# A decoder in one program: layer 2's self attention with heads split over two row groups, and layer 3's block quantisation in 16-bit pieces with a written order

## The chip, the cores and the metric

The kernel runs on one core of a Trainium2 chip. The core has five engines that work side by side, each through its own queue in order: PE (matrix multiplication; PEld is its loading of weights), DVE and ACT (element-wise work), POOL, and SP (here it only issues DMAs). SBUF is the on-chip memory of 128 partitions, PSUM the memory that PE writes. The metric is the device time of one execution in microseconds, lower is better. It was 2435.77, the median of three (2435.06 to 2436.54).

## The reference

The program computes a decoder of four layers on x of 8 blocks (b), 112 tokens and 256 features, in float32. Each layer has a self attention, a cross attention and a feed-forward part (FFN), each added to x. Two of the twelve parts matter here.

Layer 2's self attention has 8 query heads and 4 key and value heads of width 128, rotary positions and a causal mask:

```python
q = (hidden_states @ Wq).reshape(b, t, NH, D).transpose(0, 2, 1, 3)
k = (hidden_states @ Wk).reshape(b, t, NKV, D).transpose(0, 2, 1, 3)
v = (hidden_states @ Wv).reshape(b, t, NKV, D).transpose(0, 2, 1, 3)
q = q * cos + _rotate_half(q) * sin        # (-x2, x1): the halves of a head swapped
k = k * cos + _rotate_half(k) * sin
attn = jnp.einsum('bhtd,bhsd->bhts', q, k) * scale   # k, v repeated for two heads each
attn = jax.nn.softmax(jnp.where(causal, -jnp.inf, attn), axis=-1)
out = jnp.einsum('bhts,bhsd->bhtd', attn, v)
return out.transpose(0, 2, 1, 3).reshape(b, t, NH * D) @ Wo
```

Layer 3's FFN multiplies quantised values: every 16 neighbours share a scale that is rounded to an 8-bit float, and the values are rounded to eight magnitudes and a sign. Inputs and weights both are quantised so, and the hidden values once more (256 to 1024 to 256 features):

```python
amax = jnp.max(jnp.abs(xb), axis=-1, keepdims=True)          # xb: blocks of 16
sc8 = jnp.clip(amax / FP4_MAX * global_scale, 0.0, FP8_MAX).astype(float8_e4m3fn)
dq = sc8.astype(jnp.float32) / global_scale
a = jnp.clip(jnp.abs(xb) / jnp.where(dq == 0.0, 1.0, dq), 0.0, FP4_MAX)
q = jnp.sign(xb) * _FP4_VALS[jnp.digitize(a, _FP4_MIDS)]
return q * dq
...
hidden = silu(linear(x, gate_w)) * linear(x, up_w)
return linear(hidden, down_w)        # linear quantises both operands
```

## The kernel before

One class holds x in SBUF (tokens on partitions, S = 112, blocks along the free axis) through the whole program; the parts run one after the other (`SUBLAYERS`). A half is four blocks (HB = 4, HT = 448 tokens). Weights come through a ring of buffers by DMAs on SP's queue. Where nothing else is said, the Tile framework's scheduler sets the order of the instructions on each engine, within the limits of data and buffers, so that work of neighbouring parts interleaves; under `tc.manual_schedule` the order on the engines named is that of the code.

**Layer 2's self attention** (`l2_attn`, L1463 to L1512). `ln_T` normalises x and transposes it to xnT (features on partitions). Then for each half: `out` is qT (8 heads) or kT (4 heads), one chunk c of 128 partitions for each head. A chunk is a product mm of 128x448 (L407), two multiplications by sin which read the one half of the partitions and write the other (`rot`, L1487), one by cos (L1490), and POOL's addition of the two (L1491). Then each of the four blocks b: values vb, and in two groups g of four heads the scores sc (L407), mask addition, maxima and subtraction on DVE (L494, L496, L497), the exponential on ACT (L498), row sums (L1518, L1519), transposes of e (L506), the weighted values av, token-major, scaled into o (L1509), transposes of o into oT (L530), and after both groups the product with Wo and the addition to x (L484). PSUM tiles mm, sc, tr and av have two buffers each.

**The next part** (`l2_xattn`) normalises x into x1 (L445), multiplies by a gain and adds a bias (L1529, L1530, on DVE and POOL), and normalises and transposes x1. x1 stands in SBUF where qT of `l2_attn` stood, so it is written only when that tile is free.

**Layer 3's quantisation** (`quantise`, L1968) works on n values of a row, 16 neighbours a block: block maxima (L1985), nine operations on the n/16 scales (L1987 to L2001), multiplication by the inverse scale (L2004), clamping (L2005), the power of two below each value (L2007, L2008), rounding by adding and subtracting a large number (L2009, L2010), and multiplication by the scale into bfloat16 (L2011). Everything else is float32. It is used by `l3_weights` for the three weight matrices, which is dealt out as a generator inside layer 2's FFN (2048 values a row, in two calls of 1024), and by `l3_ffn` (L2060 on): on the normalised x of each half (1024 wide, result xq), and on the hidden values of two blocks at a time (2048 wide, hid into hq). Around it `l3_ffn` has the products gu (gate and up), silu on ACT (sg), hid on DVE (L2104), transposes of hq (L2113), a copy (hqT, L2117), the product y with the down weights, and the addition to x (L2121). `l0_attend` of layer 0 already works with heads of width 64 on two row groups of PE and with a written order; its lines L730 to L783 are named below because of that.

## Time and profile before

| | us |
|---|---|
| median of three runs | 2435.77 |
| lowest, highest | 2435.06, 2436.54 |
| the profiled execution, device time | 2432.16 |
| its span in the trace | 2430.4 |
| PE, DVE, ACT, POOL busy | 2138.1, 1434.3, 826.8, 215.8 |
| mean granted clock of PE | 0.954 |

All rows of the profile come from the one profiled execution; its span begins with the first and ends with the last recorded instruction. A row of the groups names line, engine, operation, output and inputs, shapes, count, busy time and mean duration, and then the engine's idle time ahead of that group with what ended it. PE's instructions overlap, so a mean duration of PE is longer than the distance from one start to the next.

### The profile page before, as it was taken

Reading aid. Unit: us, or ns where it says so; the run is one execution under the profiler, and the core shown is the slowest. Engines: PE = TensorE matmul, PEld = TensorE weight load, DVE = VectorE, ACT = ScalarE, POOL = GpSimd, SP = SyncE. Lnnn points to the kernel's source line nnn. Section 1 sums busy time; section 2 is a strip of 40 time slices with the busy share of each in tenths; the row PEclk is TensorE's granted clock in tenths of the full one; section 3 lists DMA queues with packets and bytes.
Section 4 is the critical chain, followed back from the end, with each engine's and each line's share of the span. In section 5 each row is a group of like instructions: output and inputs, shape, how many; then the busy total and the mean of one; then the engine's idle time right before and its main releaser. Section 6 shows DMA issues by size and latency. Waiting matters only on the chain.

```text
span 2430.4 us, 43101 instructions
## 1 busy us (share of the span) xinstructions
PE 2138.1 (88%) x17032; PEld 1268.6 (52%) x17032; DVE 1434.3 (59%) x3810; ACT 826.8 (34%) x2220; POOL 215.8 (9%) x415
## 2 busy tenths in 40 slices
PE   6999999889899899899988859899999999899842
PEld 3444444455556566546555536466555556556622
DVE  4555556565446567553877547767740223667698
ACT  2333334453312356430111213467321111346521
POOL 0111111000011100000222331100000000100000
PEclk9999999999999999999999979999999999899966
DMA  4000000000100000100001011000111100000000
GB/s 185 2 2 2 2 20 35 29 18 18 52 1 15 18 1 2 36 26 18 35 18 35 18 28 52 17 2 19 53 35 62 41 1 1 1 1 2 2 1 15
DMA packets 10729, 55.93 MB, mean 23 GB/s; under 512 B 1833, under 2 KB 3625, under 8 KB 5792
## 3 DMA queue, kind: packets, MB, share of 16 engines
q1 hardware_dynamic: 8304, 44.57, 5.1%
q0 software_dynamic: 2080, 7.07, 0.9%
q8 instruction: 135, 2.21, 0.4%
q10 hardware_dynamic: 144, 1.54, 0.2%
q14 instruction: 66, 0.54, 0.1%
HBM read 52.23 MB, written 0.92 MB: 22 GB/s over the span
## 4 chain that ended last, share of the span: by engine, by line
PE 66%; DVE 22%; issue 5%; ACT 4%; DMA 2%; POOL 1%; DVEq 0%; ACTq 0%; POOLq 0%
PE mm L407 31%; PE tr L1178 6%; PE gu L407 6%; PE g L640 6%; PE sc L407 4%; PE av L1194 3%; PE tr L407 1%; DVE rot L1487 1%; PE av L777 1%; ACT sg L651 1%; PE av L407 1%; ACT th L662 1%; PE s L407 1%; DVE hT L666 1%; DMA cx<-in_ctx 1%
## 5 line engine op out<-in xcount | busy, mean ns | idle before, releaser
L640 PE MATMUL g<-w,hT 128*32 128x256 f32 x3552 | 237.4, 384 | 26.0 <-DVE hT L666 24.6
L1178 PEld LDWEIGHTS tr<-cst,xe 112*125 112x125 f32 x1152 | 151.5, 188 | 96.7 <-issue 37.0
L1165 DVE TENSOR_REDUCE xnm<-sc 112x1 f32<-112x375 f32 x384 | 184.3, 540 | 29.5 <-PE sc L407 28.9
L1178 PE MATMUL tr<-cst,xe 112*125 112x112 f32 x1152 | 193.1, 289 | 8.6 <-DVE xeT L1186 3.5
L407 PE MATMUL mm<-xnT,w 128*128 128x448 f32 x432 | 183.0, 559 | 19.7 <-DVE qT L1490 4.5
L407 PE MATMUL mm<-hT,w 128*128 128x448 f32 x512 | 193.0, 539 | 0.0
L640 PEld LDWEIGHTS g<-w,hT 128*32 128x32 f32 x3552 | 95.7, 109 | 167.5 <-DVE hT L666 124.6
L407 PEld LDWEIGHTS mm<-hT,w 128*128 128x128 f32 x512 | 97.1, 190 | 94.4 <-issue 94.4
L1186 DVE COPY xeT<-tr 125x336 f32<-125x336 f32 x192 | 97.3, 507 | 70.4 <-PE tr L1178 63.0
L618 PE MATMUL g<-xw,cst 128*32 128x256 f32 x1792 | 138.7, 379 | 0.0
L1184 ACT COPY xeT<-tr 125x336 f32<-125x336 f32 x192 | 85.0, 443 | 155.8 <-PE tr L1178 155.8
L407 PE MATMUL mm<-w,hT 128*112 128x256 f32 x576 | 132.6, 389 | 0.0
L407 PEld LDWEIGHTS mm<-xnT,w 128*128 128x128 f32 x432 | 77.8, 193 | 102.8 <-issue 52.6
L1169 ACT ACTIVATE xe<-sc,xnm 112x375 f32<-112x375 f32 x256 | 126.2, 581 | 9.5 <-DVE xnm L1165 9.2
L407 PE MATMUL mm<-w,oT 128*112 128x256 f32 x416 | 105.8, 405 | 24.0 <-DVE oT L1667 15.2
L407 PE MATMUL gu<-xnT,w 128*128 128x448 f32 x320 | 124.4, 544 | 1.7 <-DVE hT L1332 1.2
L407 PEld LDWEIGHTS mm<-w,hT 128*112 128x112 f32 x576 | 103.7, 182 | 27.5 <-issue 4.8
L651 ACT ACTIVATE sg<-g 128x192 f32<-128x192 f32 x224 | 73.9, 330 | 105.4 <-PE g L640 94.1
L662 ACT ACTIVATE th<-cell 128x64 f32<-128x64 f32 x224 | 57.5, 257 | 147.2 <-DVE cell L660 147.1
L407 PEld LDWEIGHTS mm<-w,oT 128*112 128x112 f32 x416 | 73.9, 186 | 54.1 <-DVE oT L1667 16.3
L664 DVE TENSOR_TENSOR h<-sg,th 128x64 f32<-128x64 f32 x224 | 50.4, 225 | 84.8 <-ACT th L662 84.8
L2046 DVE COPY wq<-tr 128x256 bf16<-128x256 bf16 (+1 forms) x12 | 4.6, 420 | 157.5 <-PE tr L2045 157.5
(398 smaller groups left out, 3673.3 us busy)
## 6 DMA issues: line engine op xcount, KB each, us to landing
w<-in_w SPq DMA_DIRECT2D x33, 1024.0 KB, 4.9
raw<-in_wq POOLq DMA_DIRECT2D x3, 1024.0 KB, 5.3
w<-in_w SPq DMA_DIRECT2D x3, 896.0 KB, 6.4
wi<-in_wint POOLq DMA_DIRECT2D x3, 768.0 KB, 5.6
w<-in_w SPq DMA_DIRECT2D x2, 768.0 KB, 4.2
ctxT<-in_ctxT ACTq DMA_DIRECT2D x1, 1500.0 KB, 8.3
cx<-in_ctx POOLq DMA_DIRECT2D x1, 1500.0 KB, 22.5
w<-in_w SPq DMA_DIRECT2D x2, 512.0 KB, 3.5
```

Source lines behind the costliest of these rows:

```text
L407: self.nc.tensor.matmul(out, lhsT, rhs, start=i == 0, stop=i == len(pairs) - 1)
L618: nc.tensor.matmul(g[32 * j : 32 * j + 32, :], pick[:, t % 16, :], xw[:, l, t // 16, 256 * j : 256 * j + 256], start=True, stop=t == 0, sk ...
L640: nc.tensor.matmul(g[32 * j : 32 * j + 32, :], hT[l][:, c, :], whh[l][:, c, 256 * j : 256 * j + 256], start=False, stop=c == 1, skip_group ...
L651: nc.scalar.activation(sg[:, :192], g[:, :192], AF.Sigmoid)
L662: nc.scalar.activation(th, cell[l], AF.Tanh)
L664: nc.vector.tensor_tensor(h, og, th, ALU.mult)
L1165: nc.vector.tensor_reduce(nm, sc, AX.X, ALU.max, negate=True)
L1169: nc.scalar.activation(e, sc, AF.Exp, bias=nm)
L1178: nc.tensor.transpose(tp[:CH, i * S : (i + 1) * S], e[:, i * CH : (i + 1) * CH], self.ident[:S, :S])
L1184: nc.scalar.copy(eT, src)
L1186: nc.vector.tensor_copy(eT, src)
L1194: nc.tensor.matmul(avs[b][32 * j : 32 * j + 32, c * S : (c + 1) * S], values[b % 2][:CH, i, 4 * c + j, :], eTs[b, c, j][:, i, :], start=i ...
```

## The change

Two functions change their method; `l3_weights` and `_pack` on the host follow.

In `l2_attn` the columns of Wq and Wk are reordered on the host, so that a chunk of 128 partitions holds the first halves of two heads (x = 0), and the next chunk their second halves (x = 1). The rotation then combines two chunks without changing partitions, six DVE operations for a pair of chunks, with no POOL work; cos and sin for the queries are scaled by 1/sqrt(128) beforehand. A head's score is the sum of two products over 64 partitions, those of one head in partitions 0 to 63 and of the other in 64 to 127, into separate PSUM tiles (s0 to s3); the mask is added by a bfloat16 product with a unit matrix. DVE takes negated maxima; ACT's exponential takes them as bias and sums its rows; e is divided before it is transposed. Weighted values are computed feature-major (av), so that they need no transpose before the product with Wo. The order of PE, DVE and ACT is written out: half 0's six pairs stand in block 0, half 1's are dealt out in the half-steps after it, and a block's weighted values and result follow one and two blocks later. The helpers that only `l2_attn` used (`softmax_rows`, `heads_T`, `scores`, `out_T`, `self_psum`, `divided`, `row_sums`) go.

In layer 3 a block of 16 neighbours is laid out with a distance of k between its values (the host reorders the hidden features and the weights to match, and the normalisation writes xn in that order). Block maxima become a tree of four maxima over |values|, which ACT computes (Abs, `mag`); the scale s16 is bfloat16; after the multiplication the upper 16 bits of each float32 value, with the lowest bit set, are taken as bfloat16, and clamping, powers of two and rounding work on these; the result is written in two halves. `quantise` is a generator whose steps `l3_ffn` interleaves, in a written order, with the next blocks' products and the last blocks' additions to x. Weight maxima (amax in `l3_weights`) are read with the new strides.

```diff
+def _rotary(w):
+    n = w.shape[1] // P
+    a = w.reshape(w.shape[0], 2, 2, n // 4, 2, 64)
+    return a.transpose(0, 1, 3, 4, 2, 5).reshape(w.shape)
...
-        ("sin", np.concatenate([sin, -sin])),
+        ("sin", np.concatenate([sin, sin])),
...
+            def pair(half, l, i):
+                cols = slice(half * HT, (half + 1) * HT)
+                out, m = ((kT, wk), (qT, wq))[l]
+                cos, sin = turns[l]
+                parts = []
+                for x in range(2):
+                    pm = self.t(ps, [P, 512], "tr")[:, :HT]
+                    c = slice((2 * i + x) * P, (2 * i + x + 1) * P)
+                    self.mm(pm, [(m[:, k, c], self.xnT[:, k, cols]) for k in range(2)])
+                    parts.append(pm.rearrange("p (b s) -> p b s", b=HB))
+                a, b = (out[:, i, x, cols].rearrange("p (b s) -> p b s", b=HB) for x in range(2))
+                ra, rb = (self.t(acts, [P, HB, S], f"rot{x}") for x in range(2))
+                nc.vector.tensor_tensor(a, parts[0], cos, ALU.mult)
+                nc.vector.tensor_tensor(rb, parts[0], sin, ALU.mult)
+                nc.vector.tensor_tensor(ra, parts[1], sin, ALU.mult)
+                nc.vector.tensor_tensor(b, parts[1], cos, ALU.mult)
+                nc.vector.tensor_tensor(a, a, ra, ALU.subtract)
+                nc.vector.tensor_tensor(b, b, rb, ALU.add)
...
+            def score(b, p):
+                cols = slice(b * S, (b + 1) * S)
+                for r in range(2):
+                    scs[b, p, r] = self.t(ps1, [P, 512], f"s{2 * p + r}")[:S, : 2 * S].rearrange("p (h t) -> p h t", h=2)
+                    nc.tensor.matmul(
+                        scs[b, p, r].rearrange("p h t -> p (h t)"), ident, mask.rearrange("p h t -> p (h t)"),
+                        start=True, stop=False, skip_group_check=True,
+                    )
+                for i in range(2):
+                    for x in range(2):
+                        for r in range(2):
+                            rows = slice(64 * r, 64 * r + 64)
+                            nc.tensor.matmul(
+                                scs[b, p, r][:, i, :], qT[rows, 2 * p + i, x, cols], kT[rows, p, x, cols],
+                                start=False, stop=x == 1, skip_group_check=True,
                             )
-                        nc.vector.tensor_tensor(dst, src, cos, ALU.mult)
-                        nc.gpsimd.tensor_tensor(dst, dst, rot, ALU.add)
-                for j in range(HB):
-                    b = half * HB + j
-                    cols = slice(j * S, (j + 1) * S)
-                    vb = self.t(work, [P, 4, P], "vb")
-                    pm = self.t(ps, [P, 512], "mm")[:S]
-                    self.mm(pm, [(x, wv[:, k, :]) for k, x in enumerate(self.tokens(b))])
-                    self.cp(vb[:S], pm.rearrange("p (h d) -> p h d", h=4))
-                    o = self.t(work, [P, 8, P], "o")
-                    for g in range(2):
-                        hs = range(g * 4, g * 4 + 4)
-                        sc = self.scores(ps, [(qT[:, h, cols], kT[:, h // 2, cols]) for h in hs])
-                        e = self.softmax_rows(sc, work, 4, scale, self.c("causal"))
-                        ri = self.row_sums(e, 4)
-                        eT = self.heads_T(e, work, ps, 4)
-                        av = self.t(ps, [P, 512], "av")[:S].rearrange("p (h d) -> p h d", h=4)
-                        for i, h in enumerate(hs):
-                            self.mm(av[:, i, :], [(eT[:, i, :], vb[:S, h // 2, :])])
-                        nc.vector.tensor_tensor(
-                            o[:S, g * 4 : g * 4 + 4, :], av, ri[:, :, None].to_broadcast([S, 4, P]), ALU.mult
+            def maxima(b, p):
+                if p == 0:
+                    nms[b] = self.t(work, [P, 8], "nm")[:S]
+                    sus[b] = self.t(work, [P, 8], "su")[:S]
+                for r in range(2):
+                    at = 4 * p + 2 * r
+                    nc.vector.tensor_reduce(nms[b][:, at : at + 2], scs[b, p, r], AX.X, ALU.max, negate=True)
+            def exponent(b, p):
+                es[b, p] = self.t(work, [P, 4, S], f"e{p}")[:S]
+                for r in range(2):
+                    for i in range(2):
+                        h = slice(4 * p + 2 * r + i, 4 * p + 2 * r + i + 1)
+                        nc.scalar.activation(
+                            es[b, p][:, 2 * r + i, :], scs[b, p, r][:, i, :], AF.Exp,
+                            bias=nms[b][:, h], accum_out=sus[b][:, h],
                         )
-                    oT = self.out_T(o.rearrange("p h d -> p (h d)"), work, ps, 1024)
-                    self.add_to_x(b, self.project(ps, b, oT, wo))
+                    del scs[b, p, r]
+            def divide(b, p):
+                ri = self.t(self.small, [P, 4], "ri4")[:S]
+                nc.vector.reciprocal(ri, sus[b][:, 4 * p : 4 * p + 4])
+                nc.vector.tensor_tensor(es[b, p], es[b, p], ri[:, :, None].to_broadcast([S, 4, S]), ALU.mult)
...
+            def attend(b, p):
+                eT = eTs.pop((b, p))
+                av = self.t(ps1, [P, 512], "av")[:, : 4 * S]
+                for r in range(2):
+                    at = slice(2 * r * S, (2 * r + 2) * S)
+                    nc.tensor.matmul(
+                        av[:, at], vbs[b][:, 2 * p + r, :], eT[:, at], start=True, stop=True, skip_group_check=True
+                    )
+                if p == 0:
+                    oTs[b] = self.t(work, [P, 2, 4 * S], "oT")
+                (nc.vector.tensor_copy, nc.scalar.copy)[p](oTs[b][:, p, :], av)
+            def result(b):
+                oT = oTs.pop(b).rearrange("p a (i s) -> p (a i) s", i=4)
+                out = self.t(ps1, [P, 512], "mm")[:S, :D]
+                self.mm(out, [(oT[:, c, :], wo[:, c, :]) for c in range(8)])
+                self.add_to_x(b, out)
+            with tc.manual_schedule(engines={ET.PE, ET.DVE, ET.Activation}):
+                for _ in norm(0):
+                    pass
+                now = prepare(0)
+                later = chain(norm(1), prepare(1))
+                for b in range(NB + 2):
+                    on, last = b < NB, 0 < b <= NB
+                    for p in range(2):
+                        if b == 0:
+                            for _ in range(3):
+                                next(now)
+                        if on:
+                            score(b, p)
+                            maxima(b, p)
+                        if last:
+                            turn(b - 1, p)
+                        if on:
+                            exponent(b, p)
+                        if p == 0:
+                            if b > 1:
+                                result(b - 2)
+                        elif on:
+                            value(b)
+                        next(later, None)
+                        if last:
+                            attend(b - 1, p)
+                        if on:
+                            divide(b, p)
         w.done("l2a_wo")
...
+    def block_max(self, pool, src, rows, n, row):
+        nb, k = n // 16, row // 16
+        e, a = 16, src.rearrange("p (r e k) -> p r e k", e=16, k=k)
+        while e > 1:
+            e //= 2
+            out = self.t(pool, [P, nb * e], f"qm{nb * e}")[:rows]
+            o = out.rearrange("p (r e k) -> p r e k", e=e, k=k)
+            self.nc.vector.tensor_tensor(o, a[:, :, :e, :], a[:, :, e : 2 * e, :], ALU.max)
+            a = o
+        return out
...
+            amax = self.block_max(pool, mag, rows, n, row)
+            yield
+        sc, st, z, s16 = sm("s"), sm("t"), sm("z"), sm("h", BF16)
         nc.vector.tensor_scalar(sc, amax, 1.0 / 6.0, gs, ALU.mult, ALU.mult)
         nc.vector.tensor_scalar(sc, sc, 448.0, None, ALU.min)
@@ -1994,21 +2080,34 @@
         )
         nc.vector.tensor_scalar(st, st, 0.125 * big, 2.0**-9 * big, ALU.mult, ALU.max)
         nc.vector.tensor_tensor(sc, sc, st, ALU.add)
-        nc.vector.tensor_tensor(sc, sc, st, ALU.subtract)
-        nc.vector.scalar_tensor_tensor(z, sc, 0.0, sc, ALU.is_equal, ALU.add)
+        nc.vector.tensor_tensor(s16, sc, st, ALU.subtract)
+        nc.vector.scalar_tensor_tensor(z, s16, 0.0, s16, ALU.is_equal, ALU.add)
         nc.vector.reciprocal(z, z)
         nc.vector.tensor_scalar(z, z, gs, 1.0 + 2.0**-23, ALU.mult, ALU.mult)
+        yield
         a = self.t(pool, [P, n], f"qa{n}")[:rows]
-        m = self.t(pool, [P, n], f"qm{n}")[:rows]
-        nc.vector.tensor_tensor(blocks(a), blocks(src), bc(z), ALU.mult)
-        nc.vector.tensor_scalar(a, a, 6.0, -6.0, ALU.min, ALU.max)
-        nc.vector.tensor_scalar(m.bitcast(I32), a.bitcast(I32), 0x7F800000, None, ALU.bitwise_and)
-        nc.vector.tensor_scalar(m, m, 1.0, 0.5 * big, ALU.max, ALU.mult)
-        nc.vector.tensor_tensor(a, a, m, ALU.add)
-        nc.vector.tensor_tensor(a, a, m, ALU.subtract)
-        nc.vector.tensor_tensor(blocks(dst), blocks(a), bc(sc), ALU.mult)
+        b, m = (self.t(pool, [P, n], f"q{i}{n}", BF16)[:rows] for i in "bp")
+        nc.vector.tensor_tensor(wide(a), wide(src), bc(z), ALU.mult)
+        yield
+        high = a.bitcast(I16).rearrange("p (n two) -> p n two", two=2)[:, :, 1]
+        nc.vector.tensor_scalar(b.bitcast(I16), high, 1, None, ALU.bitwise_or)
+        yield
+        nc.vector.tensor_scalar(b, b, 6.0, -6.0, ALU.min, ALU.max)
+        nc.vector.tensor_scalar(m.bitcast(I16), b.bitcast(I16), 0x7F80, None, ALU.bitwise_and)
+        nc.vector.tensor_scalar(m, m, 1.0, 96.0, ALU.max, ALU.mult)
+        yield
+        nc.vector.tensor_tensor(b, b, m, ALU.add)
+        nc.vector.tensor_tensor(b, b, m, ALU.subtract)
+        yield
+        for at in range(0, n, 1024):
+            part = slice(at, at + 1024)
+            half = s16[:, at // 16 : at // 16 + 64].rearrange("p (r k) -> p r k", k=k)
+            nc.vector.tensor_tensor(
+                wide(dst[:, part]), wide(b[:, part]),
+                half[:, :, None, :].to_broadcast([rows, 64 // k, 16, k]), ALU.mult,
+            )
+            yield
...
+                mag = self.t(pool, [P, 2, 1024], "mag")[:S, 0, :]
+                nc.scalar.activation(mag, flat[0], AF.Abs)
+                for _ in self.quantise(pool, *flat, S, HB * D, D, s_in[:S], mag=mag):
+                    pass
...
+                        nc.scalar.activation(mags[b0][:, j, cols], hids[b0][:, j, cols], AF.Abs)
+                        yield
...
+            with tc.manual_schedule(engines={ET.PE, ET.DVE, ET.Activation}):
+                for _ in hidden(0):
+                    pass
+                for b0 in range(0, NB, 2):
+                    later = hidden(b0 + 2) if b0 + 2 < NB else iter(())
+                    hq = self.t(work, [P, 2, 1024], "hq", BF16)[:S]
+                    flat = [a.rearrange("p b d -> p (b d)") for a in (hids.pop(b0), hq)]
+                    mag = mags.pop(b0).rearrange("p b d -> p (b d)")
+                    for step, _ in enumerate(self.quantise(pool, *flat, S, 2048, 1024, s_down[:S], mag=mag)):
+                        if step == 1 and b0 > 0:
+                            add(b0 - 2)
+                            add(b0 - 1)
+                        if step >= 2:
+                            next(later, None)
+                        if step >= 6:
+                            result(b0 + step - 6, hq[:, step - 6, :])
+                add(NB - 2)
+                add(NB - 1)
```

## The prediction

> **What bounds it now.** I read the page first: span, busy shares, chain.
>
> ```profile
> span 2430.4 us, 43101 instructions
> PE 2138.1 (88%) x17032; PEld 1268.6 (52%) x17032; DVE 1434.3 (59%) x3810; ACT 826.8 (34%) x2220; POOL 215.8 (9%) x415
> ...
> PE 66%; DVE 22%; issue 5%; ACT 4%; DMA 2%; POOL 1%; DVEq 0%; ACTq 0%; POOLq 0%
> ```
>
> On average PE is the bound, but the average hides stages. So I read engine busy time in stretches: the first four cover layer 2's self attention, the last three layer 3's FFN (columns: length, then busy us of PE, PEld, DVE, ACT, POOL, granted clock, DMA).
>
> ```profile
> 1156.00:1184.00 28.00, 24.35 (x74) 11.29 (x74) 26.33 (x50) 2.45 (x4) 12.44 (x11) 1.00 0.15 61
> 1184.00:1232.00 48.00, 44.70 (x273) 34.64 (x272) 36.87 (x77) 11.39 (x20) 1.51 (x2) 1.00 0.00 1
> 1232.00:1258.00 26.00, 22.33 (x76) 10.81 (x74) 24.48 (x45) 0.84 (x1) 13.19 (x12) 1.00 0.12 41
> 1258.00:1303.00 45.00, 39.03 (x230) 31.81 (x231) 35.88 (x88) 14.09 (x24) 6.17 (x8) 0.92 0.07 24
> 2303.00:2335.00 32.00, 12.36 (x36) 6.42 (x35) 27.08 (x54) 5.04 (x7) 0.00 (x0) 0.56 0.00 0
> 2335.00:2384.00 49.00, 21.08 (x101) 12.53 (x100) 48.26 (x54) 11.27 (x16) 0.00 (x0) 0.74 0.00 1
> 2384.00:2431.00 47.00, 12.94 (x83) 11.36 (x80) 34.94 (x37) 4.68 (x6) 0.00 (x0) 0.61 0.06 20
> ```
>
> The self attention alternates: two rotation stretches bound by DVE (26.33 of 28, 24.48 of 26), two attention stretches bound by PE. The FFN is DVE alone (48.26 of 49). The timeline dates them: attention 1156.6 to 1304.6, next stage's first transposes 1305.7; FFN, last x add of the stage before 2306.4, first block maximum 2336.6, last quantised value 2419.1, last add 2424.5.
>
> **Part 1, self attention.** The groups of 1156 to 1304 (columns: busy, mean ns of one, idle before):
>
> ```profile
> L407 PE MATMUL mm<-xnT,w 128*128 128x448 f32 x96 | 41.4, 555 | 5.4 <-DVE qT L1490 4.5 <-DVE kT L1490 0.4 <-DVE xnT L400 0.3
> L1487 DVE TENSOR_TENSOR rot<-mm,cst 64x448 f32<-64x448 f32 x48 | 29.9, 622 | 1.7 <-PE mm L407 0.3
> L1490 DVE TENSOR_TENSOR qT<-mm,cst 128x448 f32<-128x448 f32 x16 | 10.0, 625 | 0.2
> L494 DVE TENSOR_TENSOR e<-sc,cst 112x448 f32<-112x448 f32 x16 | 9.7, 614 | 1.2 <-PE sc L407 1.2
> ```
>
> A float32 matmul is two passes (x96 for 48); mean ns overlap, so I use start to start from the timeline: 0.375 us a pass at N=448, 0.43 at 512, 0.216 at 256, 0.10 to 0.115 at 112.
>
> Rotation: before, 24 chunks of three DVE operations, 1.95 us each, 47 us, plus a POOL add each. After, 12 pairs of chunks with six DVE operations of about 0.63 (four from PSUM, two from SBUF), 4.0 with gaps: again 48 us, but half 1's six pairs are dealt out one per half-step between attention work. Their PE time, 12 x 3.0 = 36, is what it was.
>
> Attention per block b, PE: before 16 score passes 1.6, value 1.72, two sets of transposes 1.8, weighted values 1.85, result 3.46: 10.05 from one block to the next. After: scores 2 x 1.0, two mask matmuls twice 0.4, one set of transposes 0.9, values 1.72, attend 8 passes at N=224 1.6, result 3.54: about 10.2. The transposes of o and the 16 narrow matmuls are gone, the scores have twice the passes. DVE per b loses mask add, subtraction, row sum, o scaling (0.61+0.62+0.62+0.69, twice) and keeps maxima 0.76, division 0.63+0.17, one copy; ACT takes row sums with the exponentials.
>
> Sum: first rotation operation about 1159.2 (1160.8 before; half 0's copies leave DVE). Six pairs and block 0's norm of half 1, maxima and division, in order on DVE: to about 1192. Then PE is the bound, because a half-step has 9.0 of PE against 6.9 of DVE with a pair in it: b=1 to 1202.7; b=2 and 3 16.3 each, b=4 13.3, b=5 to 7 10.26 each, the two drain steps 6.5 and 3.5: 1289.9. That is 14.7 us earlier than 1304.6.
>
> Not all of it arrives. The next stage's normalisation into x1 began at 1288.74 before, under the attention's last two blocks. In the changed program x1 lies where qT lay and waits for the stage's last reader on PE (the attend of block 7) and ACT's last eT copy; on DVE's queue it stands between the last oT copy and the final x add, with all of the next norm queued behind it. That is about 1286. Then: four normalisations 2.0, gain and bias 3.6, statistics 2.3, root chain 2.5, xn 1.6, so transposes at about 1298 to 1299 against 1305.7. **Layer 2 gains about 7**; ends: 14.7 if that head stays covered, 0 or below if PE has bubbles.
>
> The price before does not show is the switch between row groups. Nearest is layer 0's attention, which does it:
>
> ```profile
> L752 ACT ACTIVATE e<-s,nm 112x112 f32<-112x112 f32 x128 | 43.9, 368 | 44.2 <-DVE nm L746 44.2
> L777 PE MATMUL av<-eT,vv 112*64 112x448 f32 x64 | 29.9, 605 | 13.7 <-DVE eT L771 12.4 <-ACT eT L771 1.2
> L737 PE MATMUL s<-kT,qT 64*112 64x112 f32 x256 | 17.5, 278 | 0.0
> ```
>
> On its timeline 16 score passes take 1.04 us (0.06 each) and PE stands 0.34 at a change of shape. A rule speaks against this change: the Trainium skill, "TensorEngine Tiling (Array Packing)", Key Properties, says that changing the tiling mode drains TensorE, while tiles run in parallel. Two changes a half-step, 16 half-steps: at 0.34 each 10.9 us, which would leave layer 2 at a loss of about 4 against the sum by the row's 1.04 plus 0.25 that I put in (+7). I take the row: L737 shows 0.0 of idle ahead of its matmuls.
>
> **Part 2, FFN.** DVE's groups of 2303 to 2431:
>
> ```profile
> L2004 DVE TENSOR_TENSOR qa<-hid,qz 112x2048 f32<-112x2048 f32 x4 | 9.2, 2292 | 0.1
> L2009 DVE TENSOR_TENSOR qa<-qa,qm 112x2048 f32<-112x2048 f32 x4 | 9.2, 2288 | 0.1
> L1985 DVE TENSOR_REDUCE qm<-hid 112x128 f32<-112x2048 f32 x4 | 9.1, 2280 | 0.0
> L2005 DVE TENSOR_SCALAR qa<-qa 112x2048 f32<-112x2048 f32 x4 | 4.9, 1224 | 0.1
> ```
>
> Before, a block: maximum 2.28, nine small operations 3.06, multiply 2.29, three one-source operations 3.67, add, subtract and scale 6.87: 18.2. After: tree of maxima 1.22+0.69+0.43+0.29 = 2.63, small ones 3.06, multiply 2.29 (float32 still), then eight operations on 16-bit data, which before does not show on SBUF. By float32 rows: `|1` 2.29 (strided), 3 x 1.22, 2 x 2.29, 2 x 1.22: block 20.95. By the skill, "VectorE: DVE Perf Modes", perf-mode tier table: at 2048 a bf16 one-source operation takes 693 ns and a bf16 tensor_tensor 1224 (float32: 1227 and 2293, which L2005 and L2009 confirm at 1224 and 2288): 1.22 + 3 x 0.69 + 2 x 1.22 + 2 x 0.69: block 15.1. The nearest row of 16-bit data, the bf16 copy L2046 of 1024 from PSUM, 686 ns, is at twice a float32 copy's rate from PSUM (448 in 0.62), so I take 15.1. The strided read of `|1` fits no 4x form; at 1x it costs 1.07 more a block.
>
> To block 0: last x add 2306.4, half 1's norm 3.9 (half 0's now lies in the stage before), two halves of xq 9.2 each (10.5 before), four hid products 3.0, then about 3 of stall, as DVE waits for ACT's Abs behind the last silu and nothing covers it; gaps 1.5: 2336.6, as before. Four blocks 60.4, twelve hid products 9.0, six x adds 2.8, gaps 2: 2410.8. The tail is one token block (transposes, copy 0.86, matmuls, add), 4.0 instead of 5.4: 2414.8 against 2424.5. Abs on ACT (about 2 a block) is hidden: ACT is busy 11.27 of 49. **Layer 3 gains about 9**, between +11 and -19 (all 16-bit work at float32 rates, stall and xq included).
>
> **Weights' quantisation.** It runs at 1727 to 1990 beside matmuls (PE about 97% busy there); DVE idles, so its gain or loss counts nothing. If cover were gone, six half-size passes, 6 x 1.5.
>
> POOL loses its 24 adds; the 49 DMA issues on SP's queue keep their order, and none of the two stages waits for one before.
>
> **Sum.** 2432.16 (the profiled execution, 0.15% below the median of 2435.77) less 16 is 2416; against the median, 2419.5.
>
> **Rivals.**
> - A, 16-bit operations run at float32 rates. Layer 3 loses 19 against 7 gained: **2448**, slower. For it: no row shows 16-bit SBUF arithmetic. Against: L2046. It decides from a block cost of 18.5, where layer 3's loss equals layer 2's gain. Chance 0.07.
> - B, PE does not stay full: switches, single PSUM buffers for scores, av and mm, and a written order that cannot step aside. Layer 0's attention has PE busy 12.27 of 14 us; the same share on the 87 us stretch adds 12.3, layer 2 nets -5: **2431.5**, half of it 2425. Against: a pair's 3.0 of matmuls and a result's 3.5 lie between dependent steps. Chance 0.18.
> - C, the next stage's head is not exposed, as its statistics of early blocks are done meanwhile: all 14.7: **2412**. Against: the wait of x1. Chance 0.17.
> - D, the main case, 2414 to 2425. Chance 0.50; 0.08 for other mishaps, both sides.
>
> Range 2407 to 2436: A's and some mishaps are left out. About 0.2% (4.9 us) can be told from no change; faster 0.84 (C, D, most of B), same 0.08, slower 0.08.
>
> **What would show it.** Right: blocks 10.2 us apart after half 1's pairs end, PE idle under 5% between 1192 and 1286; first x1 normalisation at about 1286 and transposes near 1298; bf16 rows of 0.69 and 1.22 in the FFN, a DVE stall near 3 us before block 0, 4 us from last quantised half to last add. Wrong: a score group over 1.3 us, idle PE ahead of masks, `|1` at 2.29, or a later stage that shifts the difference back, which I exclude because layer 2's FFN is bound by PE (293.5 of 301 us) and unchanged.

## The result, and the profile after

The changed kernel took 2422.41 us, the median of six runs (2418.98 to 2423.85), beside 2435.41 for the kernel before, the median of six (2427.23 to 2436.54). The ratio is 0.9945 with a 95% interval of 0.9929 to 0.996: about 13 us faster. The profiled execution took 2422.82 us. The page's span, busy shares and chain of the changed kernel:

```profile
span 2421.0 us, 43230 instructions
PE 2144.0 (89%) x17064; PEld 1268.4 (52%) x17064; DVE 1371.5 (57%) x3808; ACT 864.6 (36%) x2369; POOL 189.2 (8%) x391
PE 70%; DVE 18%; issue 5%; ACT 5%; DMA 2%; POOL 1%; DVEq 0%; ACTq 0%; POOLq 0%
```

DVE loses 63 us of work and POOL 27, ACT gains 38; DVE's share of the chain falls from 22% to 18%. Most of the removed DVE work was not on the path, since the time falls by 13. The same seven stretches as before (length; busy us of PE, PEld, DVE, ACT, POOL; granted clock; DMA):

```profile
1156.00:1184.00 28.00, 22.53 (x77) 11.45 (x76) 19.83 (x50) 6.47 (x14) 0.00 (x0) 0.94 0.20 75
1184.00:1232.00 48.00, 46.55 (x270) 30.57 (x269) 32.44 (x73) 16.61 (x70) 0.00 (x0) 1.00 0.00 1
1232.00:1258.00 26.00, 25.66 (x160) 18.39 (x159) 16.41 (x45) 11.10 (x36) 0.00 (x0) 1.00 0.12 42
1258.00:1303.00 45.00, 35.52 (x208) 26.40 (x206) 26.11 (x88) 18.12 (x61) 8.80 (x12) 0.87 0.14 47
2303.00:2335.00 32.00, 11.77 (x45) 6.28 (x44) 25.47 (x63) 12.11 (x16) 0.00 (x0) 0.70 0.00 0
2335.00:2384.00 49.00, 25.58 (x104) 16.29 (x103) 45.90 (x72) 15.91 (x24) 0.00 (x0) 0.62 0.00 1
2384.00:2431.00 47.00, 11.17 (x64) 9.26 (x64) 21.84 (x33) 5.46 (x7) 0.00 (x0) 0.62 0.07 20
```

Read the second and third rows first: the self attention no longer alternates between DVE and PE, PE is busy 46.55 of 48 and 25.66 of 26. The FFN (last three rows) is still DVE's, at 45.90 of 49, but it is through sooner. The fourth row holds what the prediction's sum had not foreseen: a granted clock of 0.87, with PE at 35.52 of 45.

Landmarks that both traces have show where the profiled 9.4 us come from. (They are less than the 13.0 of the medians because the profiled execution of before was 3.3 under its median, that of after 0.4 over.)

| landmark | before | after | difference | step |
|---|---|---|---|---|
| layer 2's self attention, first transposes | 1156.61 | 1158.38 | +1.77 | +1.77, from parts ahead of the change |
| next part, first transposes of xn | 1305.73 | 1296.06 | -9.67 | -11.44 |
| next part, first sums of eT (`su`) | 1343.42 | 1337.90 | -5.52 | +4.15 |
| transposes ahead of the second weight's maximum | 1721.66 | 1718.07 | -3.59 | +1.93 |
| transposes behind it | 1778.09 | 1776.33 | -1.76 | +1.83 |
| last x add ahead of layer 3's FFN | 2306.37 | 2304.77 | -1.60 | +0.16 |
| issue of the output's DMA | 2424.54 | 2413.89 | -10.65 | -9.05 |
| end of the span | 2430.4 | 2421.0 | -9.4 | +1.2, the output's DMA landed after 6.0 instead of 4.9 |

The two changed parts bring 11.44 and 9.05. Two things take some of it back behind the first part: +4.15 immediately, and +1.83 where the weights are quantised. The +1.77 arises ahead of the change. Whether the +1.93 is the change's stays open; more on it stands further down.

**What takes 4 us back behind the self attention.** PE's timeline of after at the join (start, us; idle before and what ended it in brackets):

```profile
1296.06 1.32 PE L480 MATMUL tr<-cst,xn 112*128 112x112 f32 x4 [7.12 <-DVE xn L457]
1298.22 1.86 PE L419 MATMUL mm<-xnT,w 128*128 128x448 f32 x2 [0.84 <-DVE xnT L1606]
```

and the same product in before:

```profile
1307.20 1.02 PE L407 MATMUL mm<-xnT,w 128*128 128x448 f32 x2 [0.84 <-DVE xnT L1537]
```

After the attention's last result, which ends at 1288.9, PE stands idle 7.12 us while DVE does the next part's norms, and then the same two passes take 1.86 instead of 1.02, although nothing about them changed. Stretches of 6 us of after give the reason in the granted clock (the last number but two):

```profile
1296.00:1302.00 6.00, 4.26 (x11) 2.40 (x12) 5.44 (x18) 0.20 (x1) 1.18 (x2) 0.50 0.00 0
1302.00:1308.00 6.00, 4.88 (x6) 1.34 (x5) 5.02 (x10) 0.31 (x1) 4.34 (x7) 0.50 0.00 0
```

The clock is half for 12 us and not full for another 6 (0.66 to 1314). In before PE waited 1.17 us at this join, and from 1302 on its clock was 1.00. Busy time has to be read with the clock beside it: at half clock the same passes keep PE busy nearly twice as long.

**What the weights take.** The timeline of after where the second weight is quantised, first the issue of its load:

```profile
1745.56 0.74 POOL L2120 DMA_DIRECT2D raw<-in_wq  x1 [12.76 <-DVE qa L2090]
...
1750.80 3.60 DVE L2124 TENSOR_REDUCE amax<-raw 128x128 f32<-128x2048 f32 x1
...
1755.24 0.21 ACT L427 ACTIVATE sd<-va 112x4 f32<-112x4 f32 x1 [3.56 <-DVE va L426]
...
1757.45 6.28 PE L419 MATMUL mm<-xnT,w 128*128 128x448 f32 x16 [3.00 <-ACT hT L1819]
```

and in before:

```profile
1752.94 0.74 POOL L2021 DMA_DIRECT2D raw<-in_wq  x1 [16.43 <-DVE qa L2004]
...
1758.08 0.20 ACT L415 ACTIVATE sd<-va 112x4 f32<-112x4 f32 x1 [1.06 <-DVE va L414]
...
1758.09 2.29 DVE L2025 TENSOR_REDUCE amax<-raw 128x128 f32<-128x2048 f32 x1
...
1760.28 4.78 PE L407 MATMUL mm<-xnT,w 128*128 128x448 f32 x12 [0.93 <-ACT hT L1750]
```

Two things are new. DVE reads the weight's maxima with the new distance between neighbours in 3.60 us (mean of three: 3.64; before, contiguous: 2.28). And the maximum has changed its place: the load waits until DVE has read the first weight for the last time (`qa`), which comes earlier because the first weight is quantised faster. So the load is issued at 1745.56 instead of 1752.94, and the maximum now stands ahead of the last block's statistics and the variance `va` on DVE's queue, where it stood behind `va` before. ACT's square root waits 3.56 for `va` (1.06 before), and the activation that PE needs comes after it: PE waits 3.00 instead of 0.93.

**Layer 3's FFN.** DVE's groups by shape (busy, mean ns of one, idle before):

```profile
L2221 DVE SCALAR_TENSOR_TENSOR hid<-gu,sc,sg 112x512 f32<-112x512 f32 x16 | 12.0, 747 | 3.4 <-ACT sg L2220 3.0
...
L2093 DVE TENSOR_SCALAR qb<-qa 112x2048 int16<-112x2048 int16 x4 | 4.9, 1221 | 0.0
...
L2100 DVE TENSOR_TENSOR qb<-qb,qp 112x2048 bf16<-112x2048 bf16 x4 | 4.9, 1217 | 0.0
...
L2095 DVE TENSOR_SCALAR qb<-qb 112x2048 bf16<-112x2048 bf16 x4 | 2.7, 686 | 0.0
```

The 16-bit operations on 2048 values take 0.69 with one source and 1.22 with two, about half of float32's 1.22 and 2.29; only `|1` (L2093), which reads every second 16-bit value, stays at 1.22. The first row's 3.0 of idle and 0.7 of waiting for ACT's Abs behind it are the stall ahead of block 0. The end of the FFN, PE's timeline:

```profile
2409.38 0.95 PE L2230 MATMUL tr<-ident,hq 112*128 112x112 bf16 x8
2411.38 1.96 PE L419 MATMUL y<-wq,hqT 128*112 128x256 bf16 x8 [1.05 <-ACT hqT L2232]
```

and in before, where one run of transposes serves both blocks:

```profile
2419.17 1.68 PE L2113 MATMUL tr<-ident,hq 112*128 112x112 bf16 x16 [12.28 <-DVE hq L2011]
```

The second token block's transposes (2409.38; its product is at 2411.38) stand in PE's written order behind the first one's product, though their input was ready at 2406.2, and ACT's copy of them then has nothing beside it. From the last quantised half to the output's DMA it is 7.7 us, against 5.4 in before: here the written order loses time that the scheduler's order did not.

### The profile page after: what moved, and what is told of

The parts are those of the page before. It is cut to its first block, busy times and chain, and to the rows that moved or that the text cites. A ratio compares the mean times of both kernels' runs of the same rounds, so it can differ in the third digit from the quotient of the medians.

```text
span 2421.0 us, 43230 instructions
## 1 busy us (share of the span) xinstructions
PE 2144.0 (89%) x17064; PEld 1268.4 (52%) x17064; DVE 1371.5 (57%) x3808; ACT 864.6 (36%) x2369; POOL 189.2 (8%) x391
## 4 chain that ended last, share of the span: by engine, by line
PE 70%; DVE 18%; issue 5%; ACT 5%; DMA 2%; POOL 1%; DVEq 0%; ACTq 0%; POOLq 0%
PE mm L419 32%; PE tr L1126 6%; PE gu L419 6%; PE g L600 6%; PE sc L419 4%; PE tr L419 3%; PE av L1142 3%; ACT sg L611 1%; PE av L737 1%; PE s L419 1%; ACT th L622 1%; DVE hT L626 1%; DMA cx<-in_ctx 1%; PE g L578 1%; DVE h L624 1%
## 5 line engine op out<-in xcount | busy, mean ns | idle before, releaser
L419 PE MATMUL mm<-xnT,w 128*128 128x448 f32 x336 | 146.4, 576 | 15.4 <-DVE qT L1095 3.6
L419 PEld LDWEIGHTS mm<-xnT,w 128*128 128x128 f32 x336 | 62.7, 198 | 78.6 <-issue 43.0
```

The lines of the kernel that those rows point to most:

```text
L419: self.nc.tensor.matmul(out, lhsT, rhs, start=i == 0, stop=i == len(pairs) - 1)
```

## The experiments

Eleven runs follow; two of them are of the same program. The medians are beside that of the kernel before in the same set of runs, whose own median went from 2432.64 to 2434.91; the ratio takes this out.

**The two parts alone: l2_only and l3_only.** One keeps layer 2's new attention with the old quantisation, activations and weights; the other the new quantisation with the old attention.

```diff
 # l2_only, against after
-    raw = [_fm(f("gate_w")[of[1]][:, of[0]]), _fm(f("up_w")[of[1]][:, of[0]]), _fm(f("down_w")[:, of[1]])]
+    raw = [_fm(f("gate_w")), _fm(f("up_w")), _fm(f("down_w"))]
-    def quantise(self, pool, src, dst, rows, n, row, gs, amax=None, mag=None):
+    def quantise(self, pool, src, dst, rows, n, gs, amax=None):
...
 # l3_only, against after
-        [("l2a_wq", _fm(_rotary(a("Wq"))))],
+        [("l2a_wq", _fm(a("Wq")))],
-        ("sin", np.concatenate([sin, sin])),
+        ("sin", np.concatenate([sin, -sin])),
```

> Only the self attention of layer 2 is the changed one; quantisation and layer 3's FFN are as before. Theory: the attention itself ends 13 us sooner after its first transposes than before, the next stage gives about 2 back by an uncovered normalisation and about 4 by a halved PE clock, and clock phases later scatter: 3 to 7 us faster than before, 2429 to 2432. Rival 'all from layer 2': 13 faster, 2422. Rival 'all from layer 3': no difference.

> Only quantisation and layer 3's FFN are the changed ones; the self attention is as before. Theory: from the last x add before the FFN to the end 109 us instead of 118, so 8 to 10 us faster than before, 2426. Rival 'all from layer 2': no difference. Together with the run of the other half the two gains should add up to the 13 of the whole change if they do not meet.

Measured: l2_only 2427.34 beside 2434.91, ratio 0.9966 (0.9953 to 0.998), 7.6 us less. l3_only 2429.76, ratio 0.9975 (0.9964 to 0.9986), 5.2 us less. The first is a little over what was expected, the second well under it. Together 12.7, so the parts add up to the whole within the noise. In l3_only the FFN itself is 9.2 us shorter (2312.61 to 2421.58 between its landmarks), but the stretch with the second weight is 3.9 longer: 9.2 - 3.9 = 5.3. In l2_only, with the old weights, that stretch is 0.2 longer. So layer 3's part gains 9 where it works and loses some of it 550 us earlier.

**PE kept busy through the gap: warm.** Nine products of no use, which change no result, are added in the attention's last drain step.

```diff
+                            if b > NB:
+                                fill = self.t(ps1, [P, 512], "s0")[:S, :HT]
+                                for _ in range(9):
+                                    nc.tensor.matmul(fill, self.c("cos"), self.xnT[:, 0, :HT], start=True, stop=True)
```

> As the changed kernel, with nine products of 112x448 whose result nobody reads put on PE behind the last result of the self attention (6.8 us of work in the 7.1 us in which PE stood idle). Theory (idle PE halves its clock): the granted clock stays near 1.00 from 1296 to 1314 instead of 0.50 to 0.66, and the point where the first block's statistics are summed comes about 4 us sooner after the attention's end; 3 to 5 us faster than the changed kernel. Rival (the clock is lowered because the attention before was dense): the clock falls all the same, and the time is the same or later by what the added products delay.

Measured: 2425.83, ratio 0.9958 (0.9943 to 0.9973): no gain over after. The same stretches of 6 us:

```profile
1290.00:1296.00 6.00, 6.00 (x22) 3.61 (x21) 6.00 (x16) 0.84 (x1) 5.63 (x8) 1.00 0.42 137
...
1302.00:1308.00 6.00, 3.70 (x8) 1.83 (x8) 5.10 (x11) 0.00 (x0) 3.31 (x5) 0.50 0.00 0
```

While the filler ran the clock stayed full, and it was 0.99 to 1302. But the next part's first write of xnT had to wait until the filler had read it, so PE then waited 2.70 us for xnT, and the clock fell to 0.50 after that. The drop was moved, not avoided: from the stage's first transposes to `su` it is 181.9 us (after: 179.5, before: 186.8). The run agrees with idle time as the cause of the slow clock, against the rival that the dense attention before it was, but it doesn't measure its price.

**x1 in a place of its own: x1_apart.** The pool that holds x1 is opened before the self attention, so that x1 no longer lies where qT lay. Nothing else changes.

```diff
-        with ExitStack() as outer:
-            keep = outer.enter_context(tc.tile_pool(name="l2x", bufs=1))
+        with self.l2x as outer:
+            keep = self.l2x_keep
...
+        if name == "l2_attn":
+            k.l2x = ExitStack()
+            k.l2x_keep = k.l2x.enter_context(tc.tile_pool(name="l2x", bufs=1))
```

> As the changed kernel, with x1 and xo of the next stage in memory of their own, so that x1 need not wait for the attention's last readers. Theory (the head of the next stage is exposed by this wait): x1 is written during blocks 5 and 6, the next stage's first transposes follow the last result within 2 us instead of 7, PE's clock stays up, and the time is 8 to 11 us under the changed kernel: 2412 to 2414. Rival (the head is bound by the DVE work itself, or DVE's earlier work delays the attention): under 3 us.

Measured: 2414.45, ratio 0.9914 (0.99 to 0.9928), 8 us under after (7.5 by the ratios). The join on PE:

```profile
1291.35 0.60 PE L480 MATMUL tr<-cst,xn 112*128 112x112 f32 x4 [0.52 <-DVE x L496]
1292.86 1.02 PE L419 MATMUL mm<-xnT,w 128*128 128x448 f32 x2 [0.91 <-DVE xnT L1606]
```

and its clock:

```profile
1302.00:1308.00 6.00, 3.93 (x13) 1.66 (x13) 5.52 (x20) 0.74 (x2) 4.55 (x7) 1.00 0.01 1
```

The early blocks' norms now run on DVE under PE's last blocks, PE waits 0.52 instead of 7.12, the two passes take 1.02 again, and the clock stays at 1.00. This prices the two losses apart. From the stage's start to the transposes it is 132.0 us against after's 137.7, so the wait cost 5.7. From the transposes to `su` it is 37.9 against 41.84, and 37.69 in before, so the slow clock cost 4. The profiled span shrank by 7.3 and not by 9.7 because the stretch with the second weight is 3.5 longer than in after: PE waits 3.49 there, and its clock falls to 0.53 behind that wait.

**The order within a score group: one_group.** Each group's products on one row group are issued one after the other, instead of changing the row group with every product.

```diff
-                for i in range(2):
-                    for x in range(2):
-                        for r in range(2):
+                for r in range(2):
+                    for i in range(2):
+                        for x in range(2):
```

> As the changed kernel, with the eight score products of a half-step ordered by row group: four of the one group, then four of the other, instead of alternating. Theory (two row groups work at the same time): a half-step's 16 passes take about 1.8 us instead of 1.04, and the blocks in the PE-bound stretch are 11.6 us apart instead of 10.1, stage longer by 8 to 12 us. Rival (a pass with half the rows is simply shorter, or PE is not the bound): 1.0 to 1.1 us and no difference.

Measured, in a single run: 2431.88. A score group of 16 passes on PE's timeline, first of after:

```profile
1202.60 1.04 PE L1506 MATMUL s<-kT,qT 64*112 64x112 f32 x16
```

then of one_group:

```profile
1216.39 1.52 PE L1506 MATMUL s<-kT,qT 64*112 64x112 f32 x16
```

The two row groups do overlap, and it takes the alternating order to have it (whether the products or the loads of their weights overlap is not separated): 0.48 a group (0.8 was expected), and blocks with two pairs are 17.04 apart instead of 16.09. With it the stage and its join are left with 0.8 of the 7.3 us of gain.

**Both ends of the FFN: ends.** The second half's input quantisation is interleaved with the first hid products, and in the tail both token blocks are transposed before either is multiplied.

```diff
+                first = hidden(0)
+                for step, _ in enumerate(rounding):
+                    if step >= 2:
+                        next(first, None)
+                turn_x(1)
...
-                            result(b0 + step - 6, hq[:, step - 6, :])
+                            turn(b0 + step - 6, hq[:, step - 6, :])
+                            if b0 + 2 < NB:
+                                product(b0 + step - 6)
+                product(NB - 2)
+                product(NB - 1)
```

> As the changed kernel, with the order of layer 3's FFN changed at its two ends: the first hidden values' products stand ahead of the second half's transposes on PE, and of the last two token blocks both are transposed before the first of their products. Theory (the head's stall and the tail are set by the written order): DVE's waits before block 0 fall from 3.7 to about 1 us, the time from the last quantised half to the last add from 7.7 to about 5, together 4 to 5 us faster than the changed kernel. Rival (the head is bound by DVE's or ACT's own work and the tail by latencies): under 2 us.

Measured: 2416.36, ratio 0.9923 (0.9908 to 0.9937), 6 us under after (5.4 by the ratios). The tail on PE's timeline:

```profile
2402.61 1.67 PE L2238 MATMUL tr<-ident,hq 112*128 112x112 bf16 x16 [9.47 <-DVE hq L2106]
2404.59 3.35 PE L419 MATMUL y<-wq,hqT 128*112 128x256 bf16 x16 [0.30 <-ACT hqT L2240]
```

One run of transposes, one run of products: 5.3 us from the last half to the DMA instead of 7.7. DVE's waits for ACT ahead of block 0 are 0.34 and 0.67 instead of 0.68, 2.29 and 0.70, and block 0 starts 24.8 after the last x add instead of 27.5. The FFN takes 104.1 us against 109.1.

**Is it the weights' quantisation: weights_before and weights_old.** weights_before reads the weights contiguously, in float32 as before, and puts the new order only into the last write. weights_old leaves that reordering out as well: each scale is then shared by other 16 weights than in the reference.

```diff
 # weights_before: the last write, reordered
+        nc.vector.tensor_tensor(
+            dst.rearrange("p (r e k) -> p r k e", e=16, k=k), a.rearrange("p (r k e) -> p r k e", e=16, k=k),
+            sc.rearrange("p (r k) -> p r k", k=k)[:, :, :, None].to_broadcast([rows, nb // k, k, 16]), ALU.mult,
+        )
...
 # weights_old: the last write, contiguous
+        nc.vector.tensor_tensor(blocks(dst), blocks(a), bc(sc), ALU.mult)
```

> As the changed kernel, but layer 3's weights are quantised by the old float32 operations on neighbouring values (the new order of the values is made by the last write), so that their block maximum is a reduction of neighbours again. Theory (the strided maximum, 3.6 us instead of 2.3, stands on DVE ahead of the statistics for which ACT's square root and then PE wait at the end of layer 2's cross attention): the wait of PE for hT there falls from 3.0 to about 1 us and the time by 2 to 4 us against the changed kernel. Rival (the weights are hidden under PE-bound work, as predicted): no difference, or slower where their longer work is not hidden.

> As the changed kernel, but layer 3's weights are quantised by all of the old operations, neighbours read and written as neighbours; it leaves out the new order of the weights' values, which the hidden and input values of the FFN keep, so that what is multiplied there isn't the reference's. Theory (the new weight quantisation is not hidden: on DVE its second maximum stands ahead of the statistics for ACT's square root, and PE waits for hT): ACT waits 1.1 us for va instead of 3.6 and PE 0.9 for hT instead of 3.0, as in both kernels with the old weights; 2 to 4 us faster than the changed kernel, 2418 to 2420. Rival (hidden, and the slower written order of the earlier run was the order and not the strides): no difference.

weights_before missed: 2423.32, ratio 0.9966 (0.9953 to 0.9979), no better than after, and the stretch is 5.8 us longer than in before. Its last write, in DVE's groups:

```profile
L2155 DVE TENSOR_TENSOR wq<-qa,qs 128x1024 bf16<-128x1024 f32 x2 | 8.9, 4462 | 0.0
```

4.46 us for what weights_old writes in 1.19: one stride was traded for a dearer one. weights_old gave 2419.7, ratio 0.9937 (0.9923 to 0.9951), and its timeline is that of before:

```profile
1760.58 4.78 PE L419 MATMUL mm<-xnT,w 128*128 128x448 f32 x12 [0.94 <-ACT hT L1819]
```

ACT waits 1.06 and PE 0.94, and the stretch is 0.06 longer than in before. So the loss at this place comes with the new weight work; the medians alone, whose intervals overlap after's, would not show it. But the run takes away two things at once, the longer maximum and its earlier place: its load is issued at 1753.24 and its maximum, of 2.29, is at 1758.50, behind `va`, as in before. apart_ends_late below moves the place alone.

**Put together: apart_ends, apart_ends_split, apart_ends_late.** apart_ends has x1_apart and ends. apart_ends_split was to cut the strided maximum in four as well; the program that ran is the same as apart_ends (its trace shows three undivided maxima of 3.61 to 3.67 us), so it is a repeat, and the split itself was not tried. apart_ends_late also makes the second weight's load wait until block 3's xn is written, by one small POOL operation:

```diff
+            if i == 1:
+                nc.gpsimd.tensor_tensor(raws[i][:S, :1], self.xn[:S, 3, :1], self.xn[:S, 3, :1], ALU.add)
             nc.gpsimd.dma_start(raws[i], self.args["in_wq"][i])
```

> x1 and xo in memory of their own and the FFN's two ends reordered, both at once, all else as in the changed kernel. If the two gains (8 us and 6 us in medians) do not meet: 2408, 27 us faster than before.

> The same, with the weights' strided maximum cut into four reductions of a quarter each, which DVE can do between other work. Theory: va stands behind three quarters of the maximum instead of all of it, so 0.5 to 1 us less for ACT's square root; 2407. Rival (four reductions cost more fixed time than they free): the same or slower.

> x1 and xo apart and the FFN's ends reordered, and the load of the second weight matrix held back until the first half of layer 2's last normalisation is written (one element of POOL ahead of its DMA), so that this matrix's strided maximum can't stand ahead of the statistics. The strides stay. Theory (it is the place on DVE's queue, not the work, that costs): ACT waits about 1 us for va instead of 3.6, PE about 0.9 for hT instead of 3.0; 2 to 4 us under the two runs of the kernel without it (2408.6 and 2407.0): 2404 to 2406. Rival: the maximum costs the same where it stands later: 2407 to 2409.

Measured: apart_ends 2408.58, ratio 0.9894 (0.9878 to 0.991), with PE's wait at the weights at 2.99; the repeat 2406.95, ratio 0.9886 (0.987 to 0.9902). apart_ends_late 2403.47 (2401.43 to 2404.79) beside 2432.64, ratio 0.9879 (0.9863 to 0.9896): PE waits 2.04 there (0.9 was expected) and the stretch is 0.86 longer than in before, against 3.4 in apart_ends. It is 29 us under the kernel before and more than twice the change's gain. The repeat differs from its twin by 1.6 us, so of the step from apart_ends to apart_ends_late (0.0015 of the time, 3.7 us) only the trace's 2.5 at that place is shown. There the maximum keeps its strides and its 3.62 us, but it is at 1745.62, behind ACT's square root at 1737.02, which waited 1.73 for `va`. So most of the loss is the place of the maximum, and not its length. Of the 2.5, 0.95 is PE's wait; the rest goes with the clock, which in apart_ends is 0.67 and 0.90 in the two slices of 4 us from 1744 on, around the end of that wait, and 1.00 here. A contiguous maximum at the early place was not tried.

## Why the prediction was right, and where its terms were off

The forecast was 16 us less in the profiled execution and 2419.5 for the median. It was 9.4 and 2422.41: direction, the main mechanism and the split between the layers held, and some terms did not, so that the size is right in part by luck.

- **Rotation no longer bounds, PE full from about 1192 to 1286.** Right: PE is busy 92.75 of these 94 us, the second block's scores start at 1191.45, blocks without a pair are 10.08 apart (10.26 predicted), with two pairs 16.09 (16.3).
- **The switch between row groups.** Right to take the row: the score groups take 1.04 as layer 0's did, and PE shows no idle ahead of the masks, and ahead of the scores only three waits for qT (1.01, 1.12 and 0.25). The rule of the Trainium skill ("TensorEngine Tiling (Array Packing)", Key Properties) that changing the mode drains TensorE has no visible price here. Its other half, tiles in parallel, agrees with one_group, where the order without alternation takes 1.52.
- **x1's normalisation at about 1286, with its transposes 12 to 13 later.** Right in place and cause: 1285.59, and x1_apart shows that qT's place was the wait. The head then took 10.5. The attention itself gained more than the sum's 14.7: from the stage's first transposes to the end of its last product it is 130.6 us against 148.0, 17.4 less. (The sum's own steps add up to 1289.4, not 1289.9, and those of layer 3 to 2336.2 ahead of block 0, not 2336.6; neither changes the forecast.) Layer 2 "gains about 7" was right to 0.3 at `su`, 7.3, by two errors that cancel: 11.44 at the transposes, and 4.15 lost to the slow clock, which no step of the sum had: it counted the head's wait once, and not what PE's clock does behind it. Rival C, whose head stays covered, is what x1_apart makes true: 16.9 at `su`.
- **Layer 3's blocks at 16-bit rates.** Right: the Trainium skill's perf-mode tier table ("VectorE: DVE Perf Modes"; 0.693 and 1.224) is met by 0.686 to 0.694 and 1.217 to 1.224, with `|1` at 1.22 as taken. Rival A is out.
- **Layer 3 "gains about 9".** 9.1, again by two errors. "2336.6, as before" for block 0 was 30.2 after the last x add; it came 27.5 after it, mostly because half 1's norm and the two halves of xq took 21.0, where the sum had 22.3 and gaps of 1.5. The stall was right, 3.7 for "about 3". And the tail is 7.7, not "4.0 instead of 5.4": the step counted one token block's work and not what stands ahead of it in PE's order, the first block's product and copy; ends shows 5.3 once that is reordered.
- **The weights, "its gain or loss counts nothing".** Wrong: +1.8 in after, +3.9 in l3_only, 5.4 in x1_apart, with the clock's part. It counted busy time beside a busy PE (261.0 of 263 us in before, so 99% and not 97%), and not the order on DVE's queue. The faster quantisation of the first weight lets the second one load earlier, and its maximum, with no urgency of its own, then stands ahead of the statistics that ACT and then PE wait for.
- **No later stage shifts the difference back.** Named as what would make it wrong, and excluded by looking at layer 2's FFN alone; the stretch that holds it indeed changes little (+0.16). The shift came in the stages between, through the clock and the weights.

Between `su` and 1718 remain +1.93. In this stretch PE has four equal waits, and the clock often falls at once or a microsecond or two behind them. The third of them in before:

```profile
1413.65 1.02 PE L1633 MATMUL s<-nT,cst 1*112 1x448 f32 x8 [2.78 <-DVE nT L1622]
```

and in after:

```profile
1408.39 1.85 PE L1702 MATMUL s<-nT,cst 1*112 1x448 f32 x8 [2.78 <-DVE nT L1691]
```

The same wait, and nearly twice the time for the same passes. From this wait to the fourth it is 14.40 us instead of 11.56, so this one fall costs 2.8; the rest of the stretch gives 0.9 back. It is not mere scatter of executions: the four other runs whose code is that of after up to here (l2_only, ends, weights_before, weights_old) show 1.85 at the same two waits, and all four runs with x1 apart show it at the first alone. But before has a single trace, and l3_only, with the old self attention, also has it at two. Whether the change sets it, and what in the program ahead does, stays open.

## What to carry to other kernels

When a stage is made faster, look at the join behind it: where the next stage's first operand lies in a buffer that the stage still reads, the gain ends at that wait, and a wait of several microseconds on PE can be paid a second time in clock, as the 7.12 us and the 4 behind them here. A change of layout has to be followed to every place that reads or writes it, also to those that run "beside" other work: what counts there is what stands behind an instruction in its queue, and making one piece of work faster can move the next one ahead of something urgent. In a written order, put all transposes of a tail ahead of the products, since the second block's ready transposes waited here behind the first block's product (ends: 5.3 us instead of 7.7).

## What the runs showed of the hardware

- **The clock after a wait of PE.** After 7.12 us of idle the granted clock was 0.50 for 12 us, though PE was busy 4.26 and 4.88 of each 6. In x1_apart it stayed at 1.00 with less busy time in the same windows (4.06 and 3.93 of 6). The work is not less, though: it is 17 and 13 recorded passes there against 11 and 6, since a pass at half clock is busy for nearly twice as long. Whether busy time or work brings the clock back is not separated by these runs. The Trainium skill, "TensorE: Matmul & The Clock Gate", Part 1, has the clock at half after an idle window of about 3.4 us, with windows that run freely. The 7.12 agrees; that waits of 2.78, shorter than such a window, are followed by a fall in seven of the eight cases of before and after, but not in the third of before (1.00 from 1412 to 1424), is more than this rule says, and no run here shows the window itself. The page also puts the warm-up's penalty under 1% of a typical span: 4 of 2422 us agrees with that, and is still a third of what the change gained.
- **Strides on DVE.** A maximum over 2048 float32 values with the 16 neighbours apart took 3.64 us against 2.28 contiguous, and a reordering write of 1024 bfloat16 values 4.46 against 1.19. The strided 16-bit read of `|1` took 1.22 where the contiguous one-source operations took 0.69, for 2048 values.
- **Row groups.** Sixteen passes over 64 partitions took 1.04 us with the row group changing at every product, and 1.52 with the four products of one group ahead of the other group's four.
